# Graph network of two layers: the last product of layer 1 made unit by unit among its groups of edges

## The chip, the core and the metric

The kernel runs on one NeuronCore of a Trainium2 chip. The metric is device time in microseconds, the median of several runs. A profile of one execution goes with it; its engines are PE (TensorE matmul), PEld (TensorE weight load), DVE (VectorE), ACT (ScalarE), POOL (GpSimd) and SP (SyncE, which here only issues DMAs).

## The reference

There are 6250 nodes with 160 features (64 scalars and 32 vectors of three) and 100000 edges, sorted by destination. Two layers of message passing follow one another, each added to its input after a LayerNorm and a ReLU:

```python
h = relu(layernorm(x)); x = x + layer0(h, edges)      # messages, sum per node, a tensor product per node
h = relu(layernorm(x)); x = x + layer1(h, edges)
# layer1:
messages = tensor_products(h[src], edge_feat) * sigmoid(edge_scalars @ W_rad.T + b_rad)
agg = segment_sum(messages, dst, n)
g = h + agg
return concat([gs @ L_s / 8, einsum('nud,uv->nvd', gv, L_v) / sqrt(32)])
```

The last lines are what the change is about: the sum of messages per node is added to `h`, multiplied by a 64x64 matrix (scalars) and a 32x32 matrix per vector component (in the kernel one 96x96 matrix), and added to `x`.

## The kernel before, in words

The main branch has these stages in order. `check` (with the first table) tests that the edges are spread evenly enough over the nodes for fixed bounds, with a slack of `SLACK` nodes; if not, a general branch would run. `scatter` makes the messages of layer 0 from tables of nodes and writes them, ordered by the other end of the edge, with indirect DMAs of GpSimd (L532). `update` sums them per node and forms the tensor product of layer 0; it leaves `xs` (the node features so far), `hs` (the normalised ones) and a table `T1` in DRAM, and clears the two tables `agg[0]`, `agg[1]`. `windows` is the edge stage of layer 1. `last` makes the final product.

`windows` works on 782 tiles of 128 edges, in 131 sets of six (`GB`). For set u:

- `gather(u)` (L982): six indirect DMAs of GpSimd fetch rows of `T1` into `wgot`, which has four buffers. It is called two sets ahead.
- `gate(u)` (L1001): two matmuls per set into PSUM (`wgate`), one set ahead; ScalarE takes their sigmoid into `wsg` (L1016). On every second set it also has SyncE fetch a piece of `wattr` and `wblk`, seven pieces ahead (L951, L954).
- `messages(u)`: ScalarE scales six tiles into PSUM (`wm`, L1013). `beside(u + 1)` copies the attributes and relative node numbers of the next set into one half of `wnear` in PSUM (L1047, L1048). VectorE makes a one-hot matrix `whot` (L1019), two products `wtc`, `wtb` (L1023, L1026) from `wnear`, adds them to `wm` (L1033, L1036) and multiplies by the gate into `wms` (L1039).
- `add(u - 1)` (L1059): six matmuls of one-hot matrix and messages into the PSUM tile `acc`. Three tiles are one window, of 32 nodes, and four windows fill the 128 partitions of `acc`. After every fourth window ScalarE copies `acc` into `wo` (L1063), and SyncE writes four blocks of 32 rows into `agg[0]` and `agg[1]` in turn, at a row that it reads into a register (L1067, L1068). Windows overlap by some nodes; neighbours go to different tables.

The order on TensorE, VectorE, ScalarE and GpSimd is that of the program, since all of it stands in a `manual_schedule` of these four engines. SyncE isn't in it: its order is planned by the compiler, and each of its DMAs waits at the head of its queue until what it needs is there. Waits are set by the framework from the accesses of each tile.

`last` comes after all sets. For 12 groups of 512 nodes and one of 106 it loads the rows of `agg[0]`, `agg[1]`, `hs` and `xs`, half of them issued by ScalarE (L286), adds the three tables with two VectorE additions per block of 128 nodes (L1106, L1107), transposes on TensorE (L263) and ScalarE (L266), multiplies (L1112, L1113), adds to the rows of `xs` (L1114) and stores (L284).

## Time and profile before

| | us |
|---|---|
| median of 3 runs (3780.93 to 3783.25) | 3781.43 |
| the profiled execution's own time | 3187.47 |
| its span, first to last instruction | 3185.7 |
| TensorE busy | 2344.3 (74%) |
| VectorE busy | 2263.5 (71%) |
| GpSimd busy | 2214.3 (70%) |
| ScalarE busy | 1513.9 (48%) |

The profiled execution is shorter than the median of the runs by 594 us. All durations below are from the profiled one. The page cuts the span into 40 slices of 79.6 us with the busy share of each engine in tenths: slices 1 to 14 are the check and `scatter`, 15 to 26 are `update`, 27 to 39 `windows` (the first gather starts at 2092 us), and the end of 39 and slice 40 hold `last`. The mean granted clock of TensorE is 0.769 of full speed.

### The profile page before, as it was taken

How to read it: one execution, taken by the hardware profiler on the slowest of the kernel's cores; microseconds unless marked ns; L12 is line 12 of the kernel's file. 1: busy time of each engine (PE TensorE's matmuls, PEld its weight loads, DVE VectorE, ACT ScalarE, POOL GpSimd, SP SyncE). 2: the span in 40 equal slices, each digit the busy share in tenths (PEclk: the TensorE clock that was granted, in tenths of full speed). 3: DMA queues.
4: the chain of work that ended last, by engine and by line, in shares of the span. 5: the costliest groups of instructions: out<-in, count | busy, mean ns of one | idle time of the engine just before them, and what ended most of it. 6: DMA issues, size and time to landing. Idle time of an engine off the chain costs nothing.

```text
span 3185.7 us, 46786 instructions
## 1 busy us (share of the span) xinstructions
PE 2344.3 (74%) x11620; PEld 1190.3 (37%) x11620; DVE 2263.5 (71%) x4660; ACT 1513.9 (48%) x5042; POOL 2214.3 (70%) x1858
## 2 busy tenths in 40 slices
PE   2677776776556459999999999966777777777658
PEld 1445454454444323333333333322333333333226
DVE  6787777776665438777777777757777777777764
ACT  1567666665555324444444444144444444444431
POOL 1577777777777738777777777757777777777740
PEclk7788878887776669999999999956655555565655
DMA  3787777776666476665565664146666666666666
GB/s 95 214 232 223 211 231 210 210 204 178 169 170 168 131 206 176 185 179 174 169 172 161 174 177 130 51 134 171 171 172 171 172 171 171 171 172 172 168 172 180
DMA packets 345348, 554.81 MB, mean 174 GB/s; under 512 B 63026, under 2 KB 244272, under 8 KB 339179
## 3 DMA queue, kind: packets, MB, share of 16 engines
q1 hardware_dynamic: 215344, 280.62, 32.0%
q0 software_dynamic: 87584, 218.31, 23.7%
q10 hardware_dynamic: 42139, 52.80, 5.1%
q8 instruction: 95, 1.56, 0.2%
q14 instruction: 186, 1.52, 0.2%
HBM read 418.48 MB, written 133.04 MB: 173 GB/s over the span
## 4 chain that ended last, share of the span: by engine, by line
PE 25%; DMA 23%; DVE 23%; POOL 11%; ACT 9%; issue 8%; SPq 1%; ACTq 0%; DVEq 0%; POOLq 0%
DMA msgs<-rec,pos_i 12%; POOL wgot L982 8%; DMA wgot<-T,src_i 7%; PE out L797 6%; DVE pr L766 4%; DVE wm L1036 3%; PE y L781 3%; POOL msgs L532 3%; ACT junk L525 3%; PE y L762 2%; DVE wtb L1026 2%; DVE wms L1039 2%; PE ptr L684 2%; PE pmsg L514 2%; DVE pr L784 2%
## 5 line engine op out<-in xcount | busy, mean ns | idle before, releaser
L532 POOL DMA_INDIRECT msgs<-rec,pos_i x782 | 777.9, 995 | 265.4 <-issue 143.0
L982 POOL DMA_INDIRECT wgot<-T,src_i x782 | 741.5, 948 | 256.2 <-issue 179.0
L514 PE MATMUL pmsg<-tw,d 120*128 120x160 f32 x1564 | 447.0, 375 | 182.3 <-ACT rec L527 182.2
L1013 ACT ACTIVATE wm<-wgot,wattr 128x160 f32<-128x160 f32 x782 | 312.3, 399 | 505.8 <-DMA wgot<-T,src_i 501.0
L1059 PE MATMUL acc<-wms,whot 128*32 128x160 f32 x1564 | 295.3, 461 | 272.6 <-DVE wms L1039 242.0
L769 POOL TENSOR_TENSOR pr<-pr 128x1500 f32<-128x1500 f32 (+1 forms) x104 | 338.2, 3252 | 157.1 <-DVE pr L766 157.1
L784 DVE TENSOR_TENSOR pr<-y,a 128x1000 f32<-128x1000 f32 (+1 forms) x312 | 352.4, 1152 | 129.3 <-PE y L781 128.5
L1001 PE MATMUL wgate<-wrad,wblk 97*128 97x480 f32 x522 | 417.0, 946 | 22.7 <-ACT wsg L1016 13.0
L514 PEld LDWEIGHTS pmsg<-tw,d 120*128 120x128 f32 x1564 | 300.0, 239 | 254.8 <-ACT rec L527 235.3
L525 ACT ACTIVATE junk<-rank,off 128x256 bf16<-128x256 f32 x782 | 372.9, 477 | 33.7 <-PE pmsg L514 7.5
L512 PE MATMUL rank<-seen,every 128*128 128x256 f16 x782 | 250.0, 320 | 169.1 <-ACT junk L525 125.8
L1059 PEld LDWEIGHTS acc<-wms,whot 128*32 128x32 f32 x1564 | 161.3, 160 | 489.6 <-ACT wm L1013 201.2
L789 POOL TENSOR_TENSOR ppr<-ppr,pr 128x1000 f32<-128x1000 f32 (+1 forms) x104 | 232.0, 2231 | 71.5 <-DVE pr L784 71.4
L527 ACT COPY rec<-pmsg 128x320 f32<-128x320 f32 x391 | 163.4, 418 | 201.8 <-DMA msgs<-rec,pos_i 190.2
L513 PE MATMUL rank<-hot,upto 128*128 128x256 bf16 x782 | 249.6, 319 | 0.8 <-DVE hot L497 0.8
L500 DVE TENSOR_TENSOR seen<-seen,hot 128x256 f16<-128x256 f16 x782 | 230.0, 294 | 27.0
L497 DVE TENSOR_SCALAR hot<-binb,qb 128x256 bf16<-128x256 bf16 x782 | 249.1, 318 | 0.0
L766 DVE TENSOR_TENSOR pr<-y,a 128x1500 f32<-128x1500 f32 (+1 forms) x104 | 172.6, 1660 | 84.6 <-PE y L762 80.3
L1036 DVE TENSOR_TENSOR wm<-wm,wtb 128x384 f32<-128x384 f32 (+1 forms) x393 | 221.7, 564 | 13.4
L1001 PEld LDWEIGHTS wgate<-wrad,wblk 97*128 97x128 f32 x522 | 145.8, 310 | 202.8 <-issue 74.8
L797 PE MATMUL out<-pr,w_f 128*64 128x500 f32 (+1 forms) x832 | 214.4, 594 | 0.0
L529 DVE CAST pos_i<-pos 128x4 int32<-128x4 f32 x196 | 44.4, 226 | 232.3 <-ACT junk L525 172.3
(205 smaller groups left out, 3945.4 us busy)
## 6 DMA issues: line engine op xcount, KB each, us to landing
urec<-msgs SPq DMA_DIRECT2D x250, 322.0 KB
attb<-in_attr SPq DMA_DIRECT2D x48, 960.0 KB
tw<-T0s SPq DMA_DIRECT2D x391, 75.0 KB
xb<-hT SPq DMA_DIRECT2D x192, 125.0 KB
dstb<-in_dstrow SPq DMA_DIRECT2D x48, 480.0 KB
T0s<-tt ACTq DMA_DIRECT2D x12, 1200.0 KB
msgs<-rec,pos_i POOLq DMA_INDIRECT x782
wgot<-T,src_i POOLq DMA_INDIRECT x782
```

What stands on the lines that cost most here:

```text
L514: nc.tensor.matmul(prs[-1][:, j % 2, :F], ds[j // WP][:, j % WP], tws[j // WP], start=True, stop=True)
L525: nc.scalar.activation(junk, rank, AF.Relu, bias=off, accum_out=pos[:, j:j + 1])
L532: nc.gpsimd.indirect_dma_start(out=views[(t0 + j) % NV][:, :], out_offset=bass.IndirectOffsetOnAxis(ap=pos_i[:, j:j + 1], axis=0), in_=rec ...
L766: nc.vector.tensor_tensor(pr[:, :, :n], y[:, i, None, :n].to_broadcast([P, 3, n]), other, op=OP.mult)
L769: nc.gpsimd.tensor_tensor(prs[0], prs[0], prs[1], op=OP.add)
L784: nc.vector.tensor_tensor(pr[:, :, :n], y[:, :, :n], a[:, j, None, :n].to_broadcast([P, 2, n]), op=OP.mult)
L797: nc.tensor.matmul(out[part, :self.n], w, pr[:, i, :self.n], start=k in self.fresh, stop=self.left[k] == 0)
L982: nc.gpsimd.indirect_dma_start(out=got[u][:, i], out_offset=None, in_=T1[:, :], in_offset=bass.IndirectOffsetOnAxis(ap=src_i[:, t0 + i:t0 ...
L1001: nc.tensor.matmul(p[:, :n], blocks[u // CH][:, u % CH], rad[:, lo * F:lo * F + n], start=True, stop=True)
L1013: nc.scalar.activation(m[:, b, j:j + F], g[:, i, oS1:oS1 + F], AF.Copy, scale=attr(u)[:, i, 0:1])
L1036: nc.vector.tensor_tensor(mv[:, :, :, 0:M0], mv[:, :, :, 0:M0], tb[:, :nt, k].rearrange("p (b t) w -> p b t w", b=h), op=OP.add)
L1059: nc.tensor.matmul(state["acc"][j:j + WN], hot[:, i], ms[:, i], start=t0 + i == w * WT, stop=t0 + i == end, tile_position=(0, j))
```

## The change

`last` is gone, and its work stands in `windows`. The nodes are cut into units of 256 (`UN` blocks of 128), 24 of them and one of 106 nodes. `fetch` is called twice per unit: first it loads the rows of `hs` and `xs`, later those of `agg[0]` and `agg[1]`, all on SyncE's queue. The second call is made once `fetchable` says that all windows still to come lie beyond the unit, by the bounds on a window's first row. `turn` transposes one block by six matmuls with the identity matrix as moving operand; it adds the three tables by accumulating in PSUM. `copies` (ScalarE), `product` (TensorE) and `close` (VectorE, and the store on SyncE after the unit's last block) follow. `finish(0)` to `finish(2)` call these at three places of each set, one block at a time, each step one set after the one before. A loop after the last set does what is left. The small tile `wnear` and the transposed block share one PSUM bank (`bank0`), `acc` and the result of the product another (`bank1`). The register with a window's first row gets narrow bounds, and `SLACK` becomes 64. That also loosens what `scatter` asks of its tables: `bounds` says how many nodes must be ready for a load.

```diff
--- before.py
+++ after.py
@@ -41,8 +41,9 @@
 OWN = 1 << 17
 NV = 16
 CH = 2
-SLACK = 96
+SLACK = 64
 CW = 4
+UN = 2
 EPS = 1e-5
@@ -970,7 +971,14 @@
             pm = s.enter_context(tc.tile_pool(name="wpm", bufs=2, space=PSUM))
             pa = s.enter_context(tc.tile_pool(name="wpa", bufs=1, space=PSUM))
             rad, blocks, attrs = e["rad"], e["blk"], e["attr"]
-            near = pa.tile([P, 2, 64], F32, name="wnear")
+            fin = s.enter_context(tc.tile_pool(name="wf", bufs=3))
+            bank0 = pa.tile([P, 512], F32, name="wbank0")
+            bank1 = pa.tile([P, 512], F32, name="wbank1")
+            near = bank0[:, 0:128].rearrange("p (a c) -> p a c", a=2)
+            ls = weight(pre, "ls", [(0, 64, c8)])
+            lv = weight(pre, "lv", [(0, 96, c32)])
             sets = [(t, min(GB, ET - t)) for t in range(0, ET, GB)]
             got, gates, ready, wrote = {}, {}, {}, []
             state = {}
@@ -1018,6 +1026,7 @@
                 hot = pool.tile([P, GB, WN], F32, name="whot")
                 nc.vector.tensor_tensor(hot[:, :nt], lane[:, None, :WN].to_broadcast([P, nt, WN]),
                                         c[:, 32:32 + nt, None].to_broadcast([P, nt, WN]), op=OP.is_equal)
+                finish(1)
                 r = c[:, :4 * GB].rearrange("p (t k) -> p t k", k=4)[:, :nt, 1:4, None]
                 tc_ = pool.tile([P, GB, 3, M1], F32, name="wtc")
                 nc.vector.tensor_tensor(tc_[:, :nt], g[:, :nt, None, oC1:oC1 + M1].to_broadcast([P, nt, 3, M1]),
@@ -1040,6 +1049,84 @@
                                         gates.pop(u)[:, :nt].rearrange("p (b t) f -> p b (t f)", b=h), op=OP.mult)
                 ready[u] = hot, ms
+            units = [(r0, min(UN * P, N - r0)) for r0 in range(0, N, UN * P)]
+            blocks_left = [(k, b) for k, (_, n) in enumerate(units) for b in range(len(blocks_of(n)))]
+            rows_in = {}
+            state.update(windows=0, loaded=0, fetched=0)
+            def fetch(k):
+                r0, n = units[k]
+                new = k not in rows_in
+                if new:
+                    rows_in[k] = {}
+                for j, src in enumerate((agg[0], agg[1], hs, xs)):
+                    if (j > 1) == new:
+                        rows_in[k][j] = t = fin.tile([P, UN, F], F32, name=f"fl{j}")
+                        transfer(nc.sync, src, t, r0, n)
+            def fetchable(k):
+                return k < len(units) and (state["windows"] == NW or
+                                           bounds(state["windows"], WT)[0] >= sum(units[k]))
+            def turn(k, b, ps):
+                rows = blocks_of(units[k][1])[b][1]
+                for lo, hi in ((0, M0), (M0, F)):
+                    for j in range(3):
+                        nc.tensor.matmul(ps[:hi - lo, lo // M0, :rows], rows_in[k][j][:rows, b, lo:hi],
+                                         ident[:rows, :rows], start=j == 0, stop=j == 2)
+            def copies(k, b, ps):
+                rows = blocks_of(units[k][1])[b][1]
+                sv = fin.tile([V, 2, P], F32, name="fT")
+                nc.scalar.copy(sv[:M0, 0, :rows], ps[:M0, 0, :rows])
+                nc.scalar.copy(sv[:, 1, :rows], ps[:V, 1, :rows])
+                return sv
+            def product(k, b, sv, p):
+                rows = blocks_of(units[k][1])[b][1]
+                nc.tensor.matmul(p[:rows, 0:M0], sv[:M0, 0, :rows], ls, start=True, stop=True)
+                nc.tensor.matmul(p[:rows, M0:F], sv[:, 1, :rows], lv, start=True, stop=True)
+            def close(k, b, p):
+                r0, n = units[k]
+                bl = blocks_of(n)
+                rows = bl[b][1]
+                x = rows_in[k][3]
+                nc.vector.tensor_tensor(x[:rows, b], x[:rows, b], p[:rows, 0:F], op=OP.add)
+                if b + 1 == len(bl):
+                    transfer(nc.sync, out, x, r0, n, store=True)
+                    rows_in.pop(k)
+            turned = bank0[:, 128:384].rearrange("p (a c) -> p a c", a=2)
+            result = bank1[:, F:2 * F]
+            def finish(i):
+                if i == 0 and "turn" in state:
+                    state["copied"] = state["turn"], copies(*state["turn"], turned)
+                    del state["turn"]
+                if i == 1 and "product" in state:
+                    close(*state.pop("product"), result)
+                if i == 2:
+                    if "copied" in state:
+                        kb, sv = state.pop("copied")
+                        product(*kb, sv, result)
+                        state["product"] = kb
+                    if blocks_left and blocks_left[0][0] < state["loaded"]:
+                        state["turn"] = blocks_left.pop(0)
+                        turn(*state["turn"], turned)
+                    state["loaded"] = f = state["fetched"]
+                    if f < len(units) and f not in rows_in:
+                        fetch(f)
+                    elif fetchable(f) and f - (blocks_left[0][0] if blocks_left else 0) < 2:
+                        fetch(f)
+                        state["fetched"] += 1
+                        if f + 1 < len(units):
+                            fetch(f + 1)
             def beside(u):
                 if u < len(sets):
                     t0, nt = sets[u]
@@ -1054,7 +1141,7 @@
                     w = (t0 + i) // WT
                     j = w % 4 * WN
                     if w % 4 == 0 and (t0 + i) % WT == 0:
-                        state["acc"] = pa.tile([P, F], F32, name="acc")
+                        state["acc"] = bank1[:, 0:F]
                     end = min((w + 1) * WT, ET) - 1
                     nc.tensor.matmul(state["acc"][j:j + WN], hot[:, i], ms[:, i], start=t0 + i == w * WT,
                                      stop=t0 + i == end, tile_position=(0, j))
@@ -1063,10 +1150,12 @@
                         nc.scalar.copy(o[:j + WN], state["acc"][:j + WN])
                         for x in range(w - w % 4, w + 1):
+                            lo, hi = bounds(x, WT)
                             with tc.issue_after(wrote[-1]) if wrote else nullcontext():
-                                row = nc.sync.value_load(base_i[0:1, x:x + 1], min_val=0, max_val=N - 1)
+                                row = nc.sync.value_load(base_i[0:1, x:x + 1], min_val=lo, max_val=hi)
                             wrote.append(nc.sync.dma_start(agg[x % 2][bass.ds(row, WN), :],
                                                            o[x % 4 * WN:x % 4 * WN + WN]).ins)
+                        state["windows"] = w + 1
             eng = mybir.EngineType
             with tc.manual_schedule(engines={eng.PE, eng.DVE, eng.Activation, eng.Pool}):
@@ -1083,36 +1172,15 @@
                     if u == 0:
                         for p, sg, n in ps:
                             nc.scalar.activation(sg, p[:, :n], AF.Sigmoid)
+                    finish(0)
                     messages(u, nxt)
                     if u:
                         add(u - 1)
+                    finish(2)
                 add(len(sets) - 1)
-
-    def last():
-
-        with tc.tile_pool(name="fw", bufs=1) as wp, tc.tile_pool(name="f", bufs=3) as pool, \
-                tc.tile_pool(name="fp1", bufs=2, space=PSUM) as pt, tc.tile_pool(name="fp2", bufs=2, space=PSUM) as pm:
-            ls = weight(wp, "ls", [(0, 64, c8)])
-            lv = weight(wp, "lv", [(0, 96, c32)])
-            for r0 in range(0, N, 4 * P):
-                n = min(4 * P, N - r0)
-                bl = blocks_of(n)
-                ts = []
-                for j, src in enumerate((agg[0], agg[1], hs, xs)):
-                    t = pool.tile([P, 4, F], F32, name=f"fl{j}")
-                    transfer(nc.sync if j % 2 else nc.scalar, src, t, r0, n)
-                    ts.append(t)
-                for b, (c, rows) in enumerate(bl):
-                    nc.vector.tensor_add(ts[0][:rows, b], ts[0][:rows, b], ts[1][:rows, b])
-                    nc.vector.tensor_add(ts[0][:rows, b], ts[0][:rows, b], ts[2][:rows, b])
-                sT = transposed(pool, pt, ts[0], bl, 0, M0, "sT")
-                vT = transposed(pool, pt, ts[0], bl, M0, F, "vT")
-                for b, (c, rows) in enumerate(bl):
-                    p = pm.tile([P, F], F32, name="pl")
-                    nc.tensor.matmul(p[:rows, 0:M0], sT[:, c:c + rows], ls, start=True, stop=True)
-                    nc.tensor.matmul(p[:rows, M0:F], vT[:, c:c + rows], lv, start=True, stop=True)
-                    nc.vector.tensor_add(ts[3][:rows, b], ts[3][:rows, b], p[:rows])
-                transfer(nc.sync, out, ts[3], r0, n, store=True)
+                while rows_in or blocks_left:
+                    for i in range(3):
+                        finish(i)
     def general():
@@ -1555,7 +1623,6 @@
             e = early(pool)
             update()
             windows(e)
-        last()
     with branch.Else():
         general()
```

## The prediction

> **What bounds the kernel now.** I read three views in this order: the page's slices, to find the stages; the table of stretches and the groups, to see which engine sets the pace of the edge stage of layer 1 (`windows`) and what stands after it; then the timeline of one set of six tiles, to find the slack of the others.
>
> ```profile
> POOL 1577777777777738777777777757777777777740
> ...
> 2400.00:2700.00 300.00, 218.25 (x641) 95.06 (x640) 232.28 (x319) 144.40 (x420) 226.81 (x241) 0.59 0.62 171
> 3071.00:3083.00 12.00, 5.92 (x28) 3.06 (x28) 9.70 (x19) 2.16 (x9) 0.82 (x1) 0.50 0.18 48
> 3083.00:3186.00 103.00, 79.40 (x294) 60.94 (x294) 38.96 (x147) 13.82 (x27) 0.00 (x0) 0.50 0.66 195
> ...
> L982 POOL DMA_INDIRECT wgot<-T,src_i x767 | 727.2, 948 | 233.9 <-issue 174.7 <-ACT wm L1013 34.5 <-DVE wms L1039 23.5
> ```
>
> The columns of the stretches are start and end, length, busy time of PE, PEld, DVE, ACT and POOL with counts, granted clock, DMA share, GB/s. In the groups (2110 to 3070 us), GpSimd's gathers take 948 ns each and 233.9/767 = 0.305 us between two, so one starts every 1.25 us whatever releaser is named. From 2092.2 us 782 of them need 979 us, to 3071: GpSimd sets the length of the stage, 7.51 us for a set of six. Then its row falls to 0, and the last 103 us are the function `last()`, the piece that the change takes away.
>
> ```profile
> 2618.81 1.16 DVE L1039 TENSOR_TENSOR wms<-wm,wsg 128x960 f32<-128x960 f32 x1
> ...
> 2620.12 2.32 PE L1059 MATMUL acc<-wms,whot 128*32 128x160 f32 x12 [1.78 <-DVE wms L1039]
> ...
> 2621.02 0.17 ACT L1048 COPY wnear<-rel 128x6 f32<-128x6 f32 x1
> 2621.12 1.02 ACT L1016 ACTIVATE wsg<-wgate 128x480 f32<-128x480 f32 x2
> 2621.22 0.35 DVE L1019 TENSOR_TENSOR whot<-lane,wnear 128x192 f32<-128x192 f32 x1 [1.25 <-ACT wnear L1048]
> 2621.50 0.76 DVE L1023 TENSOR_TENSOR wtc<-wgot,wnear 128x576 f32<-128x576 f32 x1
> ...
> 2622.17 1.35 DVE L1026 TENSOR_TENSOR wtb<-wgot,wnear 128x1152 f32<-128x1152 f32 x1
> ...
> 2622.37 3.57 PE L1001 MATMUL wgate<-wrad,wblk 97*128 97x480 f32 x4
> ```
>
> In 300 us, 40 sets, TensorE is busy 218 us, VectorE 232, ScalarE 144: per set 5.5, 5.8 and 3.6 us of 7.51. These are the slacks into which the change puts its work. The reader should also see the release of `whot`: it uses one half of `wnear`, and waits for the copy into the other half, for the set after it.
>
> [...] The clocks here (0.59 with TensorE 73% busy, 0.50 in `last()`) neither prove nor exclude that denser work would raise it; I count on no gain from it. [...]
>
> **The change, part by part.** The profiled execution took 3187.47 us, 1.8 beside its span. The median of the runs, 3781.43, is 594 us more, and no view shows where; I work in the profiled time and carry the difference over unscaled; scaled by 3781/3187 = 1.19 is an end of the range.
>
> *Removed: `last()`.* The last sum of edges (`acc`) ends at 3082.7, the span at 3185.7: 103.0 us.
>
> *TensorE, added to the stage.* 6250 nodes are 49 blocks of 128. The transposition becomes six f32 matmuls with the identity as moving operand. No row shows just that. Below: at the moved columns' rate of the gates (3.57 us / 4 records of 480 columns = 1.86 ns each at this clock), 12 records of 128 columns are 2.85 us. In `last()` a transposition is one record, 0.21 us start to start; 12 of those make 2.55, which I take (with 2.85 as the other end; at full clock half). The product is as before: L1112 and L1113 start 0.61 us apart, 1.2 per block. So 3.75 us a block, 184 us in all. A set has 3.57 + 2.35 = 5.92 at the low clock; 131 sets are 776. The sum, 960, is below 982: hidden, but with 2% to spare at the low clock (at the clock seen, 5.5 per set, 9%).
>
> *Where it waits.* `wnear` and the transposed block share one bank, `acc` and the result another. So in each of the 49 sets with a turn: the turn waits for `wtb`; behind it on TensorE stand the next gates and the next `acc`; ScalarE's two copies wait for the turn, and behind them stand the six `wm` of that set. From the end of `wnear`: to the end of `wtb` 2.3, the new add of VectorE 0.32, turn 2.55, copies 2 x 0.28 (as `wo`), six `wm` at 0.42, `wnear` 0.37: 8.6 us against 7.51. A second turn follows in the next set and has the gates (3.57), `acc` (2.35) and product (1.2) of TensorE ahead of it: turn done at 5.2 + 7.1 + 2.55 = 14.9, then 3.5 for copies, `wm`, `wnear`: 18.4, against 15.0 on schedule. So a unit puts the consumers 3.4 us behind. In the 3.3 sets of a unit without a turn TensorE and VectorE need 5.9, and regain up to 1.6 each, 5 us. GpSimd doesn't see it: four gather buffers let it run about two sets, 15 us, ahead of the release that it needs.
>
> *VectorE, ScalarE.* 49 adds of 0.32 = 16 us and 98 copies of 0.28 = 27 us, in slacks of 1.7 and 3.9 us per set. `acc` now waits for the add, which follows `whot`: some 1.5 us later than now; TensorE does it after the gates, counted above.
>
> *SyncE and DMA.* 16 MB of loads and 4 MB of stores move into 980 us: 171 to about 192 GB/s; the scatter of layer 0 moved up to 232. A unit's two table loads wait on SyncE for the landing of the window rows; behind them stand the next pieces of `wblk`/`wattr` (fetched seven ahead) and the next window rows (three `wo` buffers): both can wait 15 us. SyncE issues the fourth row 7.3 us after the first three, landing takes 2.5, the loads' issue 0.8 and landing 3 to 7: 13.6 to 17.6 us; the turn comes two sets, 15 us, later. So TensorE may wait 0 to 2.6 us a unit; I take 0.5. The loads of `ls`/`lv` and their scaling move to the stage's start, where VectorE waits 24.5 us for the first gather: nothing.
>
> *`SLACK` 96 to 64, bounds of the row register.* Nodes of layer 0 need not be quite so far ahead. No wait on the path of the chain stands on this: 0, at most 5 us either way. In the inputs of the reference the first nodes of the windows lie within -5 and +18 of an even spread, so the check still chooses the same branch.
>
> *What is late next: the new tail.* The chain of waits shows the end:
>
> ```profile
> 3082.47 3.49 DMA wagg<-wo
> ...
> 3087.59 2.52 DMA wagg<-wo
> ...
> 3090.13 6.97 DMA fl<-wagg
> ```
>
> Units 23 (two blocks) and 24 (106 nodes) can't be read before the last windows are written: landing at 3090.1 as now. Then 3.4 us for the smaller loads (between 2.5, a 20 KB row, and 7.0), three blocks in a row with turn, copies and product 2.55 + 0.8 + 1.2 = 4.6: 13.8; add 0.35; store to end of span as now, 4.9 (3180.75 to 3185.7). End at 3112.6, a tail of 29.9.
>
> *Sum:* 103.0 - 29.9 = 73 us gained. For the stage I take 8 us lost: 3.4 if the last sets are still behind, and 0.2 for each of 24 units. Net -65: 3187.5 to 3122, and 3781.4 to **3716**.
>
> **The rivals.**
> - *TensorE becomes the bound of the stage* (the slower end). The 5 us that sets without a turn could regain are not regained, because at the low clock TensorE has 2% left and stands waiting for `wtb` and loads in its own order. Then a unit costs up to 3.4 + 2.6 = 6.0 us; I take 4.5. The gain of 73 us over 24.4 units is 3.0 us a unit: above that the kernel is slower. At 4.5: 110 - 73 = +37, 3818. For it: the tight sum, and the unexplained 594 us, which could be a lower clock in the runs. Against it: 15 us of gather buffers, and mean busy of 5.5.
> - *The gathers are slowed by the moved traffic.* In the scatter of layer 0, with more traffic, GpSimd's DMA takes 995 ns, not 948: 0.047 x 782 = 37 us: 3753. Against it: there VectorE's and others' work differs too.
> - *All hidden, and the runs stretch the tail as the rest:* 73 x 1.19 = 87: 3694.
> - *The change doesn't do it:* the units aren't loaded before the end. The condition (24 x windows - 64 at or past the unit's end) holds from the 16th window on, so this is unlikely: 3781.
>
> **How the numbers follow.** Forecast 0.56 (3700 to 3740 by itself), gathers slowed 0.11, stretched 0.14, not done 0.05, TensorE 0.14. About 0.2%, 7.6 us, is what a measurement of this kernel can tell from no change. Faster: 0.56 + 0.11 + 0.14 = 0.81; same 0.05; slower 0.14. The range goes from 3692 (the stretched case) to 3785 (stage cost up to the gain); outside lie the slower case and a little below.
>
> **What would show it.** Right: the gathers still start every 1.25 us and end near 3071; after them 42 to 50 us, not 115; TensorE busy 6.5 to 7.3 us per set; `wnear` up to 3.4 us late in sets with a turn, regained after. Wrong: GpSimd waiting for `wtb` or `wm` with whole microseconds (TensorE the bound), a longer gather (traffic), TensorE waiting for `fl` loads, a span whose stage is over 1050 us, or a tail over 50 us.

## The result, and the profile after

| | before | after |
|---|---|---|
| median of 20 runs each, us | 3779.28 | 3765.86 |
| lowest, highest | 3760.06, 3789.45 | 3756.78, 3783.41 |
| the profiled execution | 3187.47 | 3770.24 |
| its span | 3185.7 | 3768.4 |

The ratio of the runs is 0.997 (95% interval 0.9957 to 0.9982): 13 us faster, not 65. The profiled execution of before that the prediction worked on took 592 us less than these runs; that of after takes what its runs take. So the two can't be subtracted. Two later executions give the pairs: the kernel before once more at 3831.8 us (c8), and the kernel after once more at 3107.9 (c5), both spans.

The gaps have a plain origin: each set of runs was made on one chip, and in three sets the kernel before took about 3185 us (medians 3184.77 to 3190.79), in five 3777 to 3825 (medians), with all runs of a set at one level. I call them the quick and the late sets. The result belongs to a late set, the profile of before to a quick one. The record gives the number of the chip for each later set: 8 was quick for c1 to c4 and late for c6 and c7. If the number names one chip, it isn't the chip alone; what it is, no run tells.

From the page of after, the slices of GpSimd and of the granted clock; `windows` begins in slice 26:

```profile
POOL 1555555565666655777777776555555555555552
PEclk7677767667666668999999999566666667666666
```

In the profile of before this row was at 7 in nearly all of `windows`; here it is at 5. The groups and stretches of after (same columns as before: start and end, length, PE, PEld, DVE, ACT, POOL, clock, DMA share, GB/s):

```profile
L990 POOL DMA_INDIRECT wgot<-T,src_i x782 | 739.6, 946 | 627.5 <-issue 420.5
```

```profile
2400.00:2700.00 300.00, 156.75 (x564) 80.58 (x564) 157.28 (x225) 107.27 (x310) 162.20 (x172) 0.64 0.47 131
3000.00:3300.00 300.00, 168.59 (x650) 93.03 (x648) 166.96 (x239) 110.22 (x323) 161.93 (x172) 0.67 0.49 137
...
3746.00:3768.00 22.00, 10.69 (x50) 8.05 (x48) 0.96 (x3) 1.51 (x7) 0.00 (x0) 0.66 0.15 40
```

A gather is as long as before (946 ns against 948), but GpSimd stands idle 627.5 us between the gathers (255.9 in c5). No engine is busy over 57% of the stage. The kernel before in a late set, two stretches of it, looks the same, but for the long end:

```profile
2500.00:2800.00 300.00, 151.51 (x482) 65.06 (x480) 173.81 (x241) 111.72 (x315) 170.07 (x180) 0.59 0.46 128
3730.00:3831.00 101.00, 79.41 (x294) 60.96 (x294) 39.01 (x147) 13.99 (x27) 0.00 (x0) 0.52 0.68 200
```

So in a late set GpSimd's own work doesn't fill this stage in either kernel (162 and 170 us of 300). What stretches it is seen in a timeline of after (start, duration, engine, line; in brackets the idle time and what ended it):

```profile
2700.96 1.87 PE L1146 MATMUL wbank<-wms,whot 128*32 128x160 f32 x12 [2.48 <-DVE wms L1048]
...
2704.69 2.64 PE L1078 MATMUL wbank<-ident,fl 128*64 128x128 f32 x10 [0.84 <-DMA fl<-wagg]
...
2713.15 0.94 POOL L990 DMA_INDIRECT wgot<-T,src_i  x1 [0.30 <-issue]
2717.40 0.29 ACT L1150 COPY wo<-wbank 128x160 f32<-128x160 f32 x1 [10.70 <-remote]
2717.62 0.26 ACT L1084 COPY fT<-wbank 64x128 f32<-64x128 f32 x1
...
2717.94 2.55 ACT L1021 ACTIVATE wm<-wgot,wattr 128x160 f32<-128x160 f32 x6
...
2720.62 0.17 ACT L1135 COPY wbank<-rel 128x6 f32<-128x6 f32 x1
...
2720.82 0.35 DVE L1027 TENSOR_TENSOR whot<-lane,wbank 128x192 f32<-128x192 f32 x1 [14.05 <-ACT wbank L1135]
...
2723.85 0.95 POOL L990 DMA_INDIRECT wgot<-T,src_i  x1 [9.76 <-issue]
```

The sum of edges ended at 2702.83 by its records, yet ScalarE's copy of it starts at 2717.40. "remote" is the profile's word where it finds no releaser in this core; the late traces hold half as many semaphore updates as the quick ones (34243 in after, 67954 in before), so their releasers are less sure. Everything behind it in ScalarE's order waits, and VectorE stands 14.05 us. Such holds of about 10 us come some 40 times in the stage; in a quick set there is none. Between them the gathers, up to four buffers ahead, are there already, and the consumers run at their own speed.

The lines of GpSimd show how a hold ends. Through it the gathers go on, one every 1.25 us, until their buffers are full; the copy starts 3.3 us after the last gather, and GpSimd then stands idle, 9.8 us in all. In c8 its pauses end with `wm`, which releases a buffer (296.5 us of waiting from 2500 to 3600 us). Counted over the traces, the waiting engines resume within such a pause of GpSimd in all 40 sets with a hold of c8, all 39 of after, 41 of 41 of c7 and 40 of 41 of c16, but only 31 of 41 of c15 (the first three sets left out). The pauses of GpSimd, idle times over 0.6 us, sum to 335 us in c8, 320 in c7, 328 in c15 and 390 in after, and to nothing in c1 and c5. That is nearly the whole of what a late stage is longer. That is an order in time; that the gathers cause the hold isn't shown by it.

Another set of the same execution, 1000 us later, with a turn and no hold, shows the consumers' speed:

```profile
3721.35 0.35 DVE L1027 TENSOR_TENSOR whot<-lane,wbank 128x192 f32<-128x192 f32 x1 [8.09 <-ACT wbank L1135]
...
3723.78 3.04 PE L1078 MATMUL wbank<-ident,fl 128*64 128x128 f32 x12 [1.87 <-DVE wtb L1035]
...
3726.91 0.26 ACT L1084 COPY fT<-wbank 64x128 f32<-64x128 f32 x1 [4.63 <-PE wbank L1078]
...
3727.22 2.55 ACT L1021 ACTIVATE wm<-wgot,wattr 128x160 f32<-128x160 f32 x6
...
3729.90 0.17 ACT L1135 COPY wbank<-rel 128x6 f32<-128x6 f32 x1
...
3730.10 0.35 DVE L1027 TENSOR_TENSOR whot<-lane,wbank 128x192 f32<-128x192 f32 x1 [2.79 <-ACT wbank L1135]
```

This is the loop of the prediction: `wtb`, turn, copies, six `wm`, `wnear`, `whot`. From `whot` to `whot` it takes 8.75 us (predicted 8.6). The gathers have ended by then (at 3715.2), so it waits for none.

The last table, made from the starts of `whot` in the timelines, tells sets with a hold (over 11 us from one start to the next) from the others, for 122 of the 131 sets (the first and last few left out). "Stage" is from the first gather to the end of the last sum of edges, "tail" from there to the end of the span.

| execution (the kernel before in its set of runs) | stage | tail | sets over 11 us, their sum | others, with a turn | others, without |
|---|---|---|---|---|---|
| before, c1 (3185) | 988.3 | 102.0 | none | | 122 x 7.50 |
| after, c5 (3188) | 988.7 | 24.6 | none | 44 x 8.08 | 78 x 7.19 |
| before, c8 (3825) | 1332.1 | 101.8 | 39, 734 | | 83 x 5.92 |
| after (3779) | 1380.3 | 22.1 | 38, 696 | 22 x 8.71 | 62 x 6.21 |
| loads alone, c7 (3778) | 1315.2 | 13.3 | 40, 724 | | 82 x 5.95 |
| after, `wnear` in `wm`, c15 (3777) | 1316.4 | 24.0 | 40, 670 | 26 x 7.10 | 56 x 6.27 |
| before, `wnear` in `wm`, c16 (3777) | 1305.0 | 102.1 | 41, 720 | | 81 x 6.02 |
| before, `wnear` in SBUF, c18 (3781) | 1222.3 | 102.7 | 29, 523 | | 93 x 6.72 |

### The profile page after: what moved, and what is told of

Its sections match the earlier page's. It is cut to its first block, busy times and chain, and to the rows that moved or that the text cites. A ratio compares the mean times of both kernels' runs of the same rounds, so it can differ in the third digit from the quotient of the medians.

```text
span 3768.4 us, 47891 instructions
## 1 busy us (share of the span) xinstructions
PE 2394.3 (64%) x12110; PEld 1269.8 (34%) x12110; DVE 2222.5 (59%) x4562; ACT 1542.2 (41%) x5114; POOL 2211.6 (59%) x1858
## 3 DMA queue, kind: packets, MB, share of 16 engines
q0 software_dynamic: 87584, 218.31, 19.9%
## 4 chain that ended last, share of the span: by engine, by line
PE 23%; another core or an unknown queue 13%; DVE 11%; ACT 7%; issue 6%; DMA 3%; POOL 1%; SPq 1%; DVEq 0%; ACTq 0%; POOLq 0%
PE out L798 5%; DVE pr L767 4%; PE wbank L1146 3%; ACT wm L1021 3%; PE y L782 3%; PE wgate L1009 2%; PE y L763 2%; PE ptr L685 2%; DMA wgot<-T,src_i 2%; PE wbank L1078 2%; DVE wtb L1035 1%; DVE pr L785 1%; PE ptr L664 1%; DVE wm L1045 1%
## 5 line engine op out<-in xcount | busy, mean ns | idle before, releaser
L990 POOL DMA_INDIRECT wgot<-T,src_i x782 | 739.6, 946 | 627.5 <-issue 420.5
L513 PE MATMUL rank<-seen,every 128*128 128x256 f16 x782 | 265.4, 339 | 536.3 <-ACT junk L526 341.1
L515 PE MATMUL pmsg<-tw,d 120*128 120x160 f32 x1564 | 475.7, 396 | 52.2 <-issue 45.6
L1146 PE MATMUL wbank<-wms,whot 128*32 128x160 f32 x1564 | 252.9, 407 | 312.5 <-ACT wo L1150 187.5
L1009 PE MATMUL wgate<-wrad,wblk 97*128 97x480 f32 x522 | 352.7, 806 | 117.2 <-issue 75.0
L1027 DVE TENSOR_TENSOR whot<-lane,wbank 128x192 f32<-128x192 f32 x131 | 45.7, 349 | 609.1 <-ACT wbank L1135 558.2
L515 PEld LDWEIGHTS pmsg<-tw,d 120*128 120x128 f32 x1564 | 323.4, 256 | 127.6 <-issue 75.3
L1146 PEld LDWEIGHTS wbank<-wms,whot 128*32 128x32 f32 x1564 | 145.3, 143 | 493.9 <-ACT wo L1150 216.6
L514 PEld LDWEIGHTS <-upto 128*128 128x128 bf16 x782 | 92.6, 118 | 620.4 <-issue 575.1
L514 PE MATMUL rank<-hot,upto 128*128 128x256 bf16 x782 | 268.0, 343 | 0.8 <-DVE hot L498 0.8
L1024 ACT ACTIVATE wsg<-wgate 128x480 f32<-128x480 f32 x259 | 137.1, 566 | 268.7 <-remote 77.9
```

Source lines behind the costliest of these rows:

```text
L513: nc.tensor.matmul(rank[:, j % 2], every, before, start=True, stop=False)
L514: nc.tensor.matmul(rank[:, j % 2], upto, hot, start=False, stop=True)
L515: nc.tensor.matmul(prs[-1][:, j % 2, :F], ds[j // WP][:, j % WP], tws[j // WP], start=True, stop=True)
L990: nc.gpsimd.indirect_dma_start(out=got[u][:, i], out_offset=None, in_=T1[:, :], in_offset=bass.IndirectOffsetOnAxis(ap=src_i[:, t0 + i:t0 ...
L1009: nc.tensor.matmul(p[:, :n], blocks[u // CH][:, u % CH], rad[:, lo * F:lo * F + n], start=True, stop=True)
L1146: nc.tensor.matmul(state["acc"][j:j + WN], hot[:, i], ms[:, i], start=t0 + i == w * WT, stop=t0 + i == end, tile_position=(0, j))
```

## The experiments

The theories, by the letters that the expectations use. **E**: what the change costs depends on what sets the pace: hidden where GpSimd does, not hidden where the consumers do. **A**: the moved hand-offs between TensorE, ScalarE and VectorE lengthen the stage (**A1** ScalarE's wait for the turn, **A2** TensorE's added time, **A3** the bank that `wnear` and the turn share). **B**, the gathers slowed by traffic; **D**, another stage; **F**, a higher clock; **H**, completions of the moved transfers.

**c1, the kernel before, unchanged.**

> The kernel before, unchanged, for a trace whose time is that of its timed runs (3779 us; the profiled execution shown before took 3187). If the change lengthened the edge stage of layer 1 (theory A): scatter and update end at the same place as in the kernel after (first gather near 2348 us), the stage from the first gather to the last sum of edges takes about 1325 us against 1398 after, and last() again about 103 us. If the loss lies elsewhere (rival D, the scatter of layer 0): the stage takes about 1398 us here too and the first gather stands near 2276. If GpSimd set the pace, as the prediction had it: gathers every 1.25 us also here, and the 594 us outside this stage.

Measured: 3179.97 us, stage 988.3, tail 102.0: the quick profile again, and this time its runs too (3184.77). The expected numbers were those of a late set, and this was none.

**c2, all units behind the last set.**

```diff
-                return k < len(units) and (state["windows"] == NW or
-                                           bounds(state["windows"], WT)[0] >= sum(units[k]))
+                return k < len(units) and state["windows"] == NW
```

> The kernel after, but no unit is loaded before the last window is written: banks, bounds and SLACK as after, no moved work beside the sets; the units come in one loop behind the last sum of edges. If the moved work lengthens the stage (A): stage back to about 1325 us, then some 49 blocks of 4.6 us = 225 us, 3900 in all. If the new places in the banks alone do it (wnear, acc and result sharing): stage still about 1398, 3975 in all.

Measured in the same set: 3230.92, ratio 1.0144 (1.0128 to 1.016). Stage 988.2, tail 145.9: three microseconds a block, since blocks overlap, not 4.6. The expectation was for a late set; here the new places in the banks alone cost the stage nothing. The bank question needed a late set.

**c3, `wnear` in SBUF.**

```diff
-            near = bank0[:, 0:128].rearrange("p (a c) -> p a c", a=2)
+            near = pre.tile([P, 2, 64], F32, name="wnear")
```

> The kernel after with wnear in SBUF, so that the turn, its copies and wnear share no bank. If the waits between wnear's readers on VectorE, the turn and the copies lengthen the stage (A): stage 1330 to 1370 us, time 3700 to 3740. If TensorE's amount of work or the traffic does (rivals): 3760 to 3775.

Measured in the same set: 3181.32, ratio 0.9981 (0.9969 to 0.9993). The tail's gain is there (19.9), but the stage is 1067.6 us, for a reason nobody had asked about: each gather has become longer.

```profile
L990 POOL DMA_INDIRECT wgot<-T,src_i x782 | 820.2, 1049 | 255.9 <-issue 209.3
```

GpSimd's idle time is as before, 255.9 us; 782 gathers of 1049 instead of 945 ns (c5) are 81 us. With the edit `whot`, `wtc` and `wtb` have both inputs in SBUF, and ScalarE's two small copies write there. That those reads of VectorE lengthen the gathers was the author's estimate from this run alone; c17 tests a part of it.

**c4, each turn made twice.** The loop over the two column ranges is run twice; the second pass overwrites the first.

> The kernel after with each transposition made twice into the same place (12 more records per block, 3.04 us; the output is unchanged). If TensorE's time stands on the path of the stage (A, and the rival that TensorE is the bound): 49 x 3.04 = 149 us more in the worst case, 3915; half of that where it only sometimes ends last, 3840. If it is hidden and only traffic (rival B) or another stage (D) took the gain: 3766 to 3775.

Measured in the same set: 3121.04, ratio 0.9797 (0.9781 to 0.9814), stage 1003.8, 15 us over that of c5 (another quick set). The expected 149 us are not what was added: the granted clock is at 7 tenths in most slices of the stage, where before has 5 and 6, and the records of the turns take 216 us in the stage, against 111 in c5. So 15 of 105 us show where GpSimd sets the pace.

**c5, the kernel after, unchanged.**

> The kernel after, unchanged, beside the kernel before on one chip. On the chip of the first four runs the kernel before took 3184.8 us and with each transposition made twice 3121.0, its gathers 1.25 us apart. Theory E: the price of the change depends on what sets the pace of the stage on the chip. Where the kernel before takes about 3185, GpSimd does, the moved work is hidden as the prediction had it, and the kernel after takes 3110 to 3120 (gathers end near 3070, a tail of 20 to 28 us). Where the kernel before takes about 3780, as in the comparison of the result, it takes about 3766, and the stage about 1380 us. Rival F: the doubled transposition itself gave the gain on that chip by a higher clock; then the kernel after takes 3150 to 3185 there.

Measured: 3106.16 against 3187.66, ratio 0.9747 (0.9734 to 0.976). The time is 4 us under E's 3110, and far from F's 3150 to 3185: E held, F fell. The lines that answer to those of before (group, then stretches):

```profile
L990 POOL DMA_INDIRECT wgot<-T,src_i x782 | 739.4, 945 | 255.9 <-issue 209.0
```

```profile
2400.00:2700.00 300.00, 217.51 (x876) 117.31 (x876) 235.22 (x333) 151.99 (x448) 226.87 (x241) 0.73 0.69 193
...
3083.00:3108.00 25.00, 12.89 (x50) 9.73 (x48) 0.96 (x3) 1.51 (x7) 0.00 (x0) 0.50 0.13 35
```

GpSimd is busy 226.87 us of 300 as before (226.81), the stage is not longer, and the tail is 24.6 us.

**c6, compute without loads,** and **c7, loads without compute,** in a late set. In c6 the fetch and the store of all but the first (and last) unit are left out; in c7 `turn`, `copies` and `product` are empty, and `close` only stores.

> The kernel after with the four loads made for the first unit alone and the store for the first and last alone; all other units take the rows of the first (so the output of the others is left out). TensorE, ScalarE and VectorE do all of the moved work. Where the kernel before takes about 3185, all is hidden behind GpSimd: 3090 to 3106, the last units not waiting for the last windows. Where it takes about 3780: theory H (the moved transfers, whose completions arrive beside the gathers', cost the stage what the tail gains) 3690 to 3710; theory A (the moved hand-offs between TensorE, ScalarE and VectorE do) 3740 to 3765.

> The kernel after with the loads and the store of every unit, but without transposition, copies, product and last addition (the last product is left out; the stored rows are those loaded). Where the kernel before takes about 3185, 3090 to 3100: the stage is GpSimd's, and the tail has three blocks less. Where it takes about 3780: theory H 3740 to 3765, theory A 3690 to 3710.

Measured: c6 3755.72, ratio 0.9928 (0.9903 to 0.9953), stage 1380.0; c7 3689.39, ratio 0.9754 (0.9723 to 0.9786), stage 1315.2. Without the transfers the stage is what it was in after, without the compute it is 65 us shorter. A holds and H falls; B falls too: a gather takes 948 ns in c7, with the transfers, as it does in before, where they stand behind the stage.

**c8 to c11, another late set.**

> The kernel before, unchanged, for its trace on the chip where it takes about 3780. If the change is hidden less there because the stage is not GpSimd's: first gather near 2367 us, a stage of 1305 to 1320 us as with the loads alone (1315.2), gathers of 946 ns but 10 us for a set, and about 103 us after the last sum of edges. If last() itself is drawn out there by as much as the rest (rival): a tail of 120 us and a stage near 1290. On a chip where it takes 3185: as in the first run of it.

Measured: 3833.56 (its runs 3825.31), stage 1332.1, tail 101.8. Taken down by the ratio of the sets' medians, 3777/3825, the stage is 1315, and the tail isn't drawn out.

In c9 `copies` returns a fixed tile of zeros:

> The kernel after without ScalarE's two copies of each transposed block; the product multiplies a fixed tile of zeros instead (so the last product is left out, its instructions are not). The transposition, the product and the last addition are issued as before, and ScalarE waits for no block. Where the kernel before takes about 3780: theory A1 (ScalarE's wait for the end of each transposition, with the six wm and the next wnear behind it, lengthens the stage) 3690 to 3715; theory A2 (TensorE's added time, wherever it is) 3745 to 3765. Where it takes 3185: 3095 to 3106.

Measured: 3749.68, ratio 0.9807 (0.9786 to 0.9828); stage 1340.8, 9 over that of c8. At 3777 this would be 3702 (an estimate by the ratio), in the range of A1.

c10 is c3 again:

> The kernel after with wnear in SBUF, once more, for the chip where the kernel before takes about 3780. Theory A3 (the shared bank: wnear's copy waits for the transposition, the transposition for wtb): 3690 to 3720, its gathers of 1050 ns not counting, since a set takes over 10 us there. A1 or A2: 3750 to 3790. Where the kernel before takes 3185: 3181 as in the run before.

Measured: 3671.28, ratio 0.9587 (0.9567 to 0.9608); stage 1254.4, with gathers of 1031 ns. Outside the expectation, on the side of A3, and more than the change's loss could give.

c11 is c4 again:

> The kernel after with each transposition made twice, once more, for the chip where the kernel before takes about 3780. Theory A2: 49 x 3.04 us = 149 more on the path, 3850 to 3915. Theory A1 or A3 (the number of waits counts, not TensorE's time): 3766 to 3800. Where the kernel before takes 3185: 3121 as in the run before.

Measured: 3853.0, ratio 1.0078 (1.0055 to 1.0101). The kernel after was not run in this set; with the result's ratio it would take 3814 (an estimate), so the doubling costs about 39 us. That is some 40% of what it adds to TensorE: by the records the turns take 237 us, against 139 in after, 98 more and not 149. The time lies between the two expectations. ScalarE's longest wait for a turn is longer too (7.8 us, against 4.6 in after, from 2500 to 3600 us), so this run alone doesn't part A1 from A2. c9 does: with the turn kept and ScalarE's wait for it gone, the stage is only 9 us over that of c8. So A2 falls as the main cause.

**c12 to c16, the bank.** `wm` is a tile of 2 x 512 columns and uses 480 of each 512. `wnear` goes into the rest of the first, so it stays in PSUM, shares a bank with its own set's `wm` and neither with the turn nor with the next set.

```diff
+                    sums[u] = m = pm.tile([P, 2, 512], F32, name="wm")
+                    c = m[:, 0, NT * F:]
-                    c = near[:, u % 2]
                     nc.scalar.copy(c[:, :4 * nt], attr(u).rearrange("p t k -> p (t k)"))
-                    nc.scalar.copy(c[:, 32:32 + nt], rel[:, t0:t0 + nt])
+                    nc.scalar.copy(c[:, 24:24 + nt], rel[:, t0:t0 + nt])
```

> The kernel after with wnear in the unused columns 480 to 511 of the first bank of its own set's wm, in PSUM still, so that it shares a bank neither with the transposed block nor with the next set's wnear, and VectorE reads it from PSUM. Theory A3 (the shared bank ate the gain): where the kernel before takes about 3780 to 3825, 3% to 4.5% below it (as 3671 of 3825 with wnear in SBUF); where it takes 3185, 3095 to 3106, with gathers of 946 ns. [...]

> The kernel before with the same place for wnear, last() unchanged. If wnear's sharing with its own other half is what costs the stage on the chip of 3780 to 3825, and the transposed block adds to it only what it adds for any other reason: 1.5% to 2.5% below the kernel before, and the moved work alone gives the rest of the run before. If only the sharing with the transposed block counts: the same time as the kernel before. Where the kernel before takes 3185: the same time, since GpSimd sets the pace.

> The kernel after, unchanged, on the same chip, for the two runs above. Where the kernel before takes 3780 to 3825: ratio 0.997 as in the result. Where it takes 3185: 3106.

This set was quick. Measured: 3107.61 (ratio 0.9746, 0.9733 to 0.9758), 3188.64 (0.9993, 0.9985 to 1.0001), 3110.81 (0.9752, 0.9738 to 0.9766): where GpSimd sets the pace none of it matters. The first two were run again, and this set was late:

> The kernel after with wnear in wm's unused columns, once more, for the chip where the kernel before takes 3780 to 3825. Theory A3 (the shared bank): 3% to 4.5% below the kernel before there, the stage 1240 to 1290 us. Rival (VectorE's reading from SBUF made the earlier run fast): ratio 0.99 to 1.00, the stage near 1380. Where the kernel before takes 3185: 3108 as before.

> The kernel before with wnear in wm's unused columns, once more, for the chip where the kernel before takes 3780 to 3825. If the old sharing (its own other half) costs the stage there: 1.5% to 2.5% below the kernel before. If only the sharing with the transposed block counts: within 0.3% of it. Where the kernel before takes 3185: within 0.1%.

Measured: c15 3711.92, ratio 0.9836 (0.9788 to 0.9885); c16 3770.45, ratio 0.9977 (0.9964 to 0.999). c15 lies short of the 3% to 4.5% that A3 expected and beyond the 0.99 of its rival; nor does `wtb` take less with `wnear` in SBUF (1354 ns in c3, 1347 in c5). So c15 is 65 us below the kernel before, 6 of which are the old sharing's: with one small tile put elsewhere, the change gives in a late set about what was predicted for it. The waits of TensorE for the turn tell what has gone. In after, from 2400 to 3700 us (line waited for, then us in total, times, longest):

```profile
PE wbank L1078 <- DVE wtb L1035: 68.8, 21, 4.0
...
PE wbank L1078 <- DMA fl<-wagg: 3.9, 2, 3.1
```

and in c15:

```profile
PE wbank L1078 <- DMA fl<-wagg: 50.7, 15, 11.7
```

The turn doesn't wait for `wtb` any more, and ScalarE waits half as long for the turn: 44.6 us from 2500 to 3600 us, against 89.7 in after, 20 times each. c9 cuts the same chain one link later. The stage is 1316.4 us against 1380.3, and a set with a turn and no hold takes 7.10 us, not 8.71. The old sharing, with the next set's half, shows in before as the wait of `whot` for the copy, 189.7 us in 123 times from 2110 to 3070 us; in a late set it is worth only the 6 us of c16.

**c17, c18.** In c17 `whot` compares `rel` where it lies in SBUF, the rest as c12; c18 is the kernel before with c3's edit.

> The kernel after with wnear in wm's unused columns, and whot comparing rel where it lies in SBUF, so that ScalarE's second small copy goes and whot waits for none of ScalarE's writes. Where the kernel before takes 3185: if an operation of VectorE with both sources in SBUF slows GpSimd (the reading of the run with wnear in SBUF, gathers 1049 against 945 ns), only whot does it here, 0.35 of 2.47 us: gathers near 960 ns and 3110 to 3125; if it is one of the longer products, 945 ns and 3108. Where it takes 3780 to 3825: 2% to 4.5% below it, 1.6% being the wnear in wm and 4.1% the wnear in SBUF.

> The kernel before with wnear in SBUF. Where the kernel before takes 3185: the gathers slow to 1049 ns, the stage 1065 us, 3262. Where it takes 3780 to 3825: if whot's waits for ScalarE (wnear's other half or wm) cost the stage there apart from the change, 2% to 2.5% below, and the change then gives the rest of the 4.1%; if not, within 0.3%.

Measured in a late set: c17 3697.55, ratio 0.977 (0.9735 to 0.9806); c18 3688.31, ratio 0.9751 (0.9727 to 0.9776). In c17 the gathers stay at 947 ns:

```profile
L990 POOL DMA_INDIRECT wgot<-T,src_i x782 | 740.2, 947 | 571.4 <-issue 368.7
```

So it isn't `whot` that lengthens them in c3, c10 and c18 (1049, 1031, 1018): it has both inputs in SBUF in c17 too and leaves them at 947, where c12 has 945. What c3, c10 and c18 have besides is `wtc` and `wtb`, 0.76 and 1.35 us long, with both inputs in SBUF, and the small copies of ScalarE into SBUF, 0.33 us a set. That it is the two products is the author's estimate from these lengths; no run parts them from the copies. And 2.5% of c10's 4.1% was there to be had without the change (c18, whose slower gathers go with 29 sets over 11 us, not 39 to 41; why is open): 0.9751 x 0.9836 = 0.959, c10's 0.9587. Of the versions run, `wnear` in `wm` (c12, c15) is the one to keep: in a late set faster than both kernels, in a quick one as fast as the kernel after. Whether c17 is better still isn't settled: its interval overlaps that of c15, and it had no quick set.

## Why the prediction was wrong

The step that failed: "The median of the runs, 3781.43, is 594 us more, and no view shows where; I work in the profiled time and carry the difference over unscaled." The 594 us lie where they do harm to the sum. c8 beside c1: the first gather at 2397.9 instead of 2087.9, the stage 1332.1 instead of 988.3, the tail 101.8 instead of 102.0. Over half of the difference of the two executions (654 us) lies inside the stage whose slack was to hide the work, and there "GpSimd sets the length of the stage, 7.51 us for a set of six" isn't true. Nor is it the lower clock that the prediction thought of: a record of the gates takes 879 ns in c8 and 946 in before, on the pages. Taken by its steps:

- **The removed tail:** predicted 103.0 - 29.9 = 73. Measured 102 to 22.1 and 24.6, so 77 to 80. The new tail is shorter because unit 23 can be read before the last window is written: its first turn comes 5.4 us after the last sum, not 10.8. A block in a row takes 4.70 us (predicted 4.6), the last addition to the end 4.9. From the timeline of after:

```profile
3745.17 1.12 PE L1146 MATMUL wbank<-wms,whot 128*32 128x160 f32 x4 [0.40 <-ACT wo L1150]
...
3751.72 3.07 PE L1078 MATMUL wbank<-ident,fl 128*64 128x128 f32 x12 [5.43 <-DMA fl<-wagg]
...
3756.42 3.07 PE L1078 MATMUL wbank<-ident,fl 128*64 128x128 f32 x12
...
3763.18 0.32 DVE L1098 TENSOR_TENSOR fl<-fl,wbank 106x160 f32<-106x160 f32 x1 [2.17 <-PE wbank L1091]
```

- **TensorE:** the turn of a block of 128 takes 3.04 us where the granted clock is 0.50 (predicted 2.55, other end 2.85), at 2513.67 and 3059.30 us of after, and 1.67 where it is 1.00, at 2535.68 and 3040.38. In a quick set all of it is hidden, as predicted (a stage of 988.7 us in c5, 988.3 in c1).
- **The bank, 8.6 against 7.51:** the mechanism was right (in after the turn waits for `wtb` 68.8 us, in 21 times, and `acc` for the add 32.2, in 14), and so was its size (8.71 without a hold). Its cost was not: "regained in sets without a turn" holds in c5, where those take 7.19 us and those with a turn 8.08, 7.51 in the mean. In a late set there is nothing to regain from. The sets between holds already run at 5.92 us, the consumers' own pace, to make up for the holds, so what a set with a turn takes more is lost, unless a hold covers it. Against the loads alone the 122 sets of the table lose (22 x 8.71 + 62 x 6.21) - 82 x 5.95 = 89 us, and sets with a hold take 28 less; 61 in all. The stage as a whole takes 1380.3 - 1315.2 = 65.
- **The sum of a late set:** about 79 gained at the end and 65 lost to the moved compute make 14, where 13 are measured. The kernel before has no trace from the set of the result, so this is put together from other late sets.
- **SyncE, traffic, `SLACK`:** nothing, as taken. The first gather starts at 2366.0 in after and 2365.0 in c16; the stage of c6, without the loads, is as long as that of after; a gather takes 946 ns, in before 948. The rival of slower gathers falls.
- **TensorE as the bound:** falls. It is busy 56% in the stage, c9 and c15 keep its turns and lose little, and of the 98 us that its doubled turn adds 39 show.
- **Predicted signs:** gathers "every 1.25 us" and a set at 7.5: right in c5, wrong in after. TensorE busy "6.5 to 7.3 us per set": wrong even in c5 (217.5 us in 40 sets, 5.4 each), at a granted clock of 0.73 where before has 0.59. After the last gather "42 to 50 us": 36 in c5, 53 in after. "A span whose stage is over 1050 us" and GpSimd waiting with whole microseconds were the signs of a wrong forecast, and they came; but the bound that they point to isn't TensorE.

In a quick set, the level of the profile that the prediction worked on, the change gives 81.5 us (3187.66 to 3106.16), and the prediction's 65 errs mostly by the 8 us charged for the stage and the shorter tail.

**What stays open** is the hold itself: why a result of TensorE that is complete by its records is taken up some 10 us late, on some sets of runs and not on others, with the same program. The traces show the lost time in `scatter` (1024 us from first to last indirect DMA in before, 1295 in after) and in `windows`, not in `update` (973 and 976 us between them): in the two stages where GpSimd makes indirect DMAs. The gathers' own duration doesn't change (948 ns in before and c8). TensorE's records get no longer in `windows` (a gate 946 ns in before, 879 in c8) and some 5% longer in `scatter` (`pmsg` 375 and 393). Nothing was tried against the hold; fewer gather buffers, or gathers further apart, would test whether it hangs on them. That c15 shortens the stage by taking the bank away is measured; that the missing catch-up is the reason is worked out from the timelines, and no run isolates it.

## What to carry to other kernels

When the profiled time and the timed runs differ by more than the change is worth, find the place of the difference first, or forecast for both cases: slack against the pacing engine is slack only in the execution that has that pace. Hide work where it takes up no place in the chain of the consumers, so that it doesn't matter which pace holds: here, in a late set, one PSUM bank shared with a tile of that chain cost about 54 us (3765.86 in after, 3711.92 in c15), and unused columns of another tile's bank gave them back. Before moving a tile from PSUM to SBUF, see what becomes of GpSimd's work beside it: here the gathers took 1049 ns instead of 945, and where they set the pace the stage was 79 us longer (c3 beside c5).

## What the runs showed of the hardware that was not expected

- One program took 3185 us in some sets of runs and 3777 to 3825 in others, each set steady within 1%, with gathers of the same length (948 ns in before and c8); the difference is waits for results that are there by the records. The lost time lies in the two stages with GpSimd's indirect DMAs, and in `windows` the waits end when these pause: in c8 in all 40 cases counted.
- With `wnear` in SBUF instead of PSUM GpSimd's gathers took 1049 ns (c3), 1031 (c10) and 1018 (c18), against 945 (c5); VectorE's products then have both inputs in SBUF, and ScalarE's small copies write there. A short comparison with both inputs there (`whot`, 0.35 us) left them at 947 (c17).
- With the moved work TensorE's records got shorter: in c5 the granted clock in the stage is 0.73, not the 0.59 of before, a record of the gates takes 796 ns instead of 946, one of the sums 381 instead of 461, and TensorE is busy 217.5 us in 300 with 876 records, where before has 218.3 with 641. With the turns doubled (c4) a record of the gates takes 731. So the moved work partly paid for itself, a gain that the prediction refused to count on; what raises the clock no run shows.
